# Counting edges into three tables in turn, halving the searches, and moving divisions and mixtures one site up in a graph-network kernel

## The chip, the core and the metric

The kernel runs on one core of one Trainium2 chip. The core has a matrix engine (TensorE, PE in the profile), a vector engine (VectorE, DVE), an activation engine (ScalarE, ACT), a general engine (GpSimd, POOL) and a sync engine (SyncE, SP) that here only issues transfers. Each engine works through its own instructions in order and waits for the others by semaphores. GpSimd and SP also issue DMAs; all of them share 16 DMA engines. The metric is the device time of one execution in microseconds (us); less is better. Three runs of the kernel before took 736.06, 737.99 and 738.41 us.

## What is computed

Two graph layers on 384 nodes and 12672 edges, each on a normalised and rectified copy of x, each added back to x. The first is a masked attention of 16 heads; its mask is set edge by edge. The second is a relational convolution of two layers, and there the count of edges by relation and node divides the messages:

```python
h = jnp.maximum(_layernorm(x), 0.0)
x = x + attention(h, edge_index, edge_type_5, ...)     # q, k, v: two projections each; mask.at[src, dst].set(w[edge_type - 1])
h = jnp.maximum(_layernorm(x), 0.0)
x = x + rgcn(h, edge_index, edge_type_6, ...)

def _rgcn_conv(x, src, dst, edge_type, basis, comp, root, bias):
    W = jnp.einsum('rb,bio->rio', comp, basis)          # R = 6 relations, B = 4 bases
    h_all = jnp.einsum('ni,rio->rno', x, W)
    counts = jnp.zeros((R, n), x.dtype).at[edge_type, dst].add(1.0)
    norm = 1.0 / counts[edge_type, dst]
    msg = h_all[edge_type, src] * norm[:, None]
    agg = jax.ops.segment_sum(msg, dst, num_segments=n)
    return agg + x @ root + bias
```

`rgcn` projects h by `w_in` (1024 to 768), applies this twice, each time with a rectifier, a residual and a batch norm, and projects back by `w_out` with a layer norm. All data are float32.

## The kernel before

The kernel turns gathering and scattering into dense matrices. For every relation r it builds a matrix A[r] of 384 x 384 that counts the edges from each source to each destination; a column divided by its sum is the mean of the relation. For each basis b the matrix At[b] is the mixture of the six divided matrices with the weights `comp[r, b]`; the convolution then is the sum over b of (x times basis b) times At[b].

**Building the tables.** The edges come as 99 chunks of 128. Two edges of one chunk must not write the same cell in one DMA, so each chunk is searched on VectorE: `find_cells` (L232) loads the keys of some chunks, shifts them (`cells`, L241), and for each chunk compares the 128 keys with each other (L250, one instruction and one read of its accumulator, 0.27 us in all). It does so twice: `find(0, ...)` for the mask and `find(1, ...)` for the counts, each closed by two short instructions (L253, L255) that give the places of the writes. The chunks are dealt into pieces (`PIECES`); pieces 0 to 2 are searched ahead, pieces 3 to 9 at the steps 3, 6, 8, 10, 12, 14 and 16 of a generator, `edge_steps`. Its steps are called from the projections by `fill(1)` (L404, L483): step 3 in the last part of the first projection, step n + 4 in part n of the 16 later parts (four of each of q2, k, k2 and v). `find_cells` does the first search and returns the second as a function; L296 calls it on the spot.

GpSimd writes each chunk: `put_mask` (L260) into one of four mask tables, `put_count` (L264) into one of two count tables `atab` in DRAM, as a DMA that adds to what is there. Such a DMA has to wait until an earlier one on the same table has landed. Counts 0 to 10 go to table 0, the others in turn to both. From count 20 on nothing but counts is left on GpSimd (L300), and they run on through the attention into the second layer. `clear` (L270) fills a table's relations with zeros through SP ahead of that.

**The projections.** Each of the 16 parts makes 7 products of half the width (a scheme that saves an eighth product by sums of operands): per part VectorE makes four sums of weights for the next part (`prepare`, L371), then whatever `fill` brings, then adds products from PSUM (L496, L502, L504); the last product of a part, `rest`, runs two products into the next one, and it writes the bank `pa` that L502 reads. At the end of a projection `node_sum` makes four sums of the new operand (L364).

**The end of the attention.** At f + 2 == STEPS (L647) SP loads the input projection and five parts of the first two bases, and then A: for each relation a plain load from one table (SP for relations 0 and 1, GpSimd for the others) and a load from the other that adds (L658). `add_up(r)` (L330) sums the three blocks of rows of A[r] on GpSimd.

**The convolution.** Each layer runs over four bases (`for b in range(B)`, L832) and then the root (L875). In a basis TensorE runs three steps c of twelve matrix instructions (3.87 us), with the `rest` of the basis before after step 0 (1.94 us), and then four products (7.74 us). `go_between(l, b, c)` (L822) is called after each step and, as c = 4, at the basis' end; what runs there is looked up in `between` (L811). Two kinds of work stand there. `share(r)` (L335): one matmul with ones (two matrix instructions) gives the column sums, VectorE takes the maximum with 1 and the reciprocal (L340, L341), GpSimd multiplies A[r] (L342), then `add_up(r + 2)`. `mix(l, r, At, bs)` (L319): for r = 0 on ScalarE, else one VectorE instruction over 128 x 1152 per basis (L326). On VectorE the site's work of step 2 comes before the sums L853, L861 and L863 that empty the banks of the basis, and `weight_sums` of the next basis (L787, L789) comes after them and before the site c = 4. The first matmuls of the next basis write the bank that L861 reads; the third block of the root's first row writes the one that L853 reads.

Of the kernel before, what the change touches and what calls it, by code (L numbers as in the profile page):

```python
# [10 lines left out]
F32 = mybir.dt.float32  # L11
# [19 lines left out]
R = 6  # L31
# [20 lines left out]
def gnn_kernel(ctx: ExitStack, tc: tile.TileContext, out, x, edges, chunks, cols, rows, small,  # L52
# [114 lines left out]


    mtab = [tables.tile([MCELLS + P, 1], F32, name=f"mtab{i}") for i in range(MT)]
    atab = [tables.tile([ACELLS + P, 1], F32, name=f"atab{i}") for i in range(2)]  # L170
    keys_d = tables.tile([PAD, P], I32, name="keys_d")

    def edge_steps(ep, none, zero):
# [58 lines left out]
        def find_cells(p):  # L232

            r0, r1 = PIECES[p:p + 2]
            nt = tables_in(r0)
            keys, cells = [ep.tile([P, MT * 3, P], I32, tag=tag, name=tag, bufs=bufs)[:, :nt * (r1 - r0)]
                           for tag, bufs in (("keys", 3), ("cells", 1))]
            nc.sync.dma_start(keys.rearrange("p (j c) n -> p j (c n)", j=nt),
                              keys_d.rearrange("(j c) n -> j (c n)", j=MT)[None, :nt, r0 * P:r1 * P]
                              .to_broadcast([P, nt, (r1 - r0) * P]))  # L240
            nc.vector.tensor_scalar(cells, keys, 3, None, ALU.logical_shift_right)  # L241

            def rounds(v):
                return v.rearrange("p (j c) -> p j c", j=MT)[:, :nt, r0:r1]

            def find(i, row, mine, times, least):
                for n in range(nt * (r1 - r0)):
                    c = n // (r1 - r0) * PER + r0 + n % (r1 - r0)
                    same = ep.tile([P, P], F32, tag="same", name="same", bufs=2)
                    nc.vector.scalar_tensor_tensor(same, row[:, n, :], mine[:, c:c + 1], times,  # L250
                                                   ALU.is_equal, ALU.mult, accum_out=count[:, i, c:c + 1])
                off = ep.tile([P, MT, 3], F32, tag="off", name="off", bufs=2)[:, :nt, :r1 - r0]
                nc.vector.scalar_tensor_tensor(off, rounds(count[:, i, :]), least, rounds(away[:, i, :]),  # L253
                                               ALU.is_ge, ALU.mult)
                nc.vector.tensor_tensor(rounds(at[:, i, :]), off, rounds(own[:, i, :]), ALU.add)  # L255

            find(0, cells, own[:, 0, :], later, 1.0)
            return lambda: find(1, keys, key, weigh, 1024.0)
# [4 lines left out]

        def put_count():  # L264
            i, c = next(counts)
            nc.gpsimd.indirect_dma_start(atab[0 if i < 18 - DEALT else i % 2][:, :],  # L266
                                         bass.IndirectOffsetOnAxis(at[:, 1, c:c + 1], 0),
                                         count[:, 1, c:c + 1], None, compute_op=ALU.add)

# [18 lines left out]
            put_rounds(p)  # L288
        for find_more in rest:
            find_more()  # L290
        for step in range(2, 18):
            yield
            for i in {5: (0,), 6: (1,), 7: (2, 3), 8: (4, 5)}.get(step, (step - 4,) if 10 <= step < 16 else ()):
                clear(i // R, i % R)
            if step in (3, 6, 8, 10, 12, 14, 16):
                find_cells(max(3, step // 2 + 1))()  # L296
            for p in {8: (3,), 9: (4,), 10: (5,), 11: (6,), 16: (7, 8), 17: (9,)}.get(step, ()):
                put_rounds(p)
        yield
# [30 lines left out]
    def add_up(r):  # L330
        sums[r] = late.tile([P, N], F32, tag="sum", name="sum", bufs=2)
        nc.gpsimd.tensor_tensor(sums[r], A[:, r, 0, :], A[:, r, 1, :], ALU.add)
        nc.gpsimd.tensor_tensor(sums[r], sums[r], A[:, r, 2, :], ALU.add)

    def share(r):  # L335

        ps = next_bank("ps_cnt", ring[1:])
        nc.tensor.matmul(ps[:, :N], ones, sums[r], start=True, stop=True)
        rn = late.tile([P, N], F32, tag="rn", name="rn", bufs=2)
        nc.vector.tensor_scalar(rn, ps[:, :N], 1.0, None, ALU.max)  # L340
        nc.vector.reciprocal(rn, rn)  # L341
        nc.gpsimd.tensor_tensor(A[:, r], A[:, r], rn[:, None, :].to_broadcast([P, NT, N]), ALU.mult)  # L342
        if r + 2 < R:
            add_up(r + 2)


    with ExitStack() as inner:
# [284 lines left out]
        for g in range(STEPS + 1):  # L632
            f = g + LEAD
            if g < STEPS:
                turn_probs(g)
            if f < STEPS:
                exponents(f)
            if f - 1 in total:
                normalise(f - 1)
            if f + 1 < STEPS:  # L640
                scores(f + 1)
            if g == STEPS:
                ps_y = [next_bank("ps_y", range(7)) for _ in range(2)]
                multiply_o(ps_y[0], 0, 0, range(KD - 1))
            if g > 0:
                gather(g - 1)
            if f + 2 == STEPS:  # L647

                w_x = [act_tile("w_x") for _ in range(2)]
                for half in range(2):  # L650
                    nc.sync.dma_start(w_x[half], w_in[half])
                tabs = [tab[:ACELLS, :].rearrange("(t p r d) o -> r p t (d o)", p=P, r=R, t=NT) for tab in atab]
                w_first = [wload(basis[0, 0, part], "w_c") for part in range(3)]
                w_first += [wload(basis[0, 1, part], "w_c") for part in range(2)]
                for r in range(2):
                    nc.sync.dma_start(A[:, r], tabs[0][r])
                for r in range(R):
                    nc.gpsimd.dma_start(A[:, r], tabs[1][r], accum_op=ALU.add)  # L658
                    if r + 2 < R:
                        nc.gpsimd.dma_start(A[:, r + 2], tabs[0][r + 2])  # L660
                    if 0 < r < 3:
                        add_up(r - 1)
        soft_stack.close()
        xtp = ctx.enter_context(tc.tile_pool(name="xtp", bufs=2, side="right"))

# [100 lines left out]
    with tc.tile_pool(name="conv", bufs=1) as cp:  # L766
# [38 lines left out]
        def shares(*rs):  # L805
            return lambda: [share(r) for r in rs]

        def mixes(l, r, *bs):
            return lambda: mix(l, r, At, bs)

        between = {(0, 1, 1): shares(0), (0, 1, 2): shares(1),  # L811
                   (0, 2, 0): lambda: (mix(0, 0, At), share(2)), (0, 2, 1): mixes(0, 1, 0, 1), (0, 2, 2): mixes(0, 1, 2, 3),
                   (0, 2, 4): shares(3),
                   (0, 3, 0): mixes(0, 2, 0, 1), (0, 3, 1): lambda: (mix(0, 2, At, (2, 3)), share(4)),
                   (0, 3, 2): mixes(0, 3, 0, 1), (0, 3, 4): shares(5),
                   (0, 4, 0): mixes(0, 4, 0, 1), (0, 4, 1): mixes(0, 5, 0, 1), (0, 4, 2): mixes(0, 3, 2, 3),
                   (0, 4, 3): mixes(0, 4, 2, 3), (0, 4, 4): mixes(0, 5, 2, 3),
                   (1, 0, 0): mixes(1, 0, 0, 1, 2, 3)}
        for i in range(10):
            between[1, (i + 1) // 3, (i + 1) % 3] = mixes(1, 1 + i // 2, *((0, 1), (2, 3))[i % 2])  # L820
# [311 lines left out]
```

## Time and profile before

| | us |
|---|---|
| median of three runs | 737.99 |
| the profiled execution, its time | 735.77 |
| its span in the profile | 734.0 |
| TensorE busy | 713.5 (97%) |
| VectorE busy | 472.9 (64%) |
| GpSimd busy | 323.3 (44%) |
| projections of half width (16 parts) | 55.39 to 209.80 |
| attention proper | from 237.4 to 310.7 |
| convolution, layer 0: bases | 384.7 to 471.9 |
| last count issued by GpSimd | 385.05 |
| first matmul of a `share` | 413.55 |

A span is what the profile shows between the first and the last instruction; the time of the execution holds 1.8 us more around it. Busy shares are means over the whole: TensorE is busy nearly always, while VectorE is nearly full in some stretches (19.9 of 20 us between 445 and 465) and idle in others. Times in the text are from the start of the span. In the profile, a row of a timeline gives start, duration, engine, line, operation, output and inputs and, in brackets, how long the engine was idle before and who released it. A row of the waits gives who waited for whom, the total, how often, and the longest.

### The profile page before, as it was taken

The page shows a single profiled execution, that of the slowest core. Times are in us where ns is not written, and L with a number is a line of the kernel's source. Part 1 is how long each engine was busy: PE and PEld are TensorE (multiplying, and loading weights), DVE is VectorE, ACT ScalarE, POOL GpSimd, SP SyncE. Part 2 cuts the span into 40 slices and gives each one's busy share as a digit, 9 for nine tenths or more (in the row PEclk, how much of TensorE's full clock was granted, in tenths as well). Part 3 has the DMA queues.
Part 4 walks back from the last instruction along what each step waited for, and adds up shares of the span by engine and source line. Part 5 has one row for each costly group of instructions (what it writes and reads, how often), then busy time and mean ns, then how long its engine had stood idle before and what let it go on. Part 6 is the DMA issues. An engine that isn't in the chain of part 4 may idle for free.

```text
span 734.0 us, 8299 instructions
## 1 busy us (share of the span) xinstructions
PE 713.5 (97%) x3024; PEld 496.8 (68%) x3024; DVE 472.9 (64%) x1228; ACT 147.2 (20%) x338; POOL 323.3 (44%) x242
## 2 busy tenths in 40 slices
PE   8999989999999999999999999899999999999995
PEld 8759989999964444445995555555555555579943
DVE  6895897877504499625424779990187676506756
ACT  3201111111111477510131131100013111001100
POOL 1456777788886788587784454310000000030000
PEclk9999999999999999999999999999999999999999
DMA  7797766743447322623527953321003123700001
GB/s 296 261 346 231 221 182 209 212 148 115 116 119 240 59 1 2 215 0 47 127 2 169 312 163 129 129 83 46 0 1 107 66 85 129 271 29 1 1 29 57
DMA packets 40533, 90.96 MB, mean 124 GB/s; under 512 B 19644, under 2 KB 27680, under 8 KB 36270
## 3 DMA queue, kind: packets, MB, share of 16 engines
q1 hardware_dynamic: 18478, 79.62, 30.9%
q0 software_dynamic: 21008, 8.42, 10.4%
q10 hardware_dynamic: 1008, 2.41, 0.9%
q8 instruction: 23, 0.38, 0.2%
q14 instruction: 16, 0.13, 0.1%
HBM read 79.27 MB, written 11.16 MB: 123 GB/s over the span
## 4 chain that ended last, share of the span: by engine, by line
PE 86%; DVE 11%; ACT 1%; issue 1%; DMA 1%; DVEq 0%; ACTq 0%
PE ps_g L846 13%; PE ps_g L840 10%; PE ps_c L897 6%; PE ps_c L880 6%; PE ps_q L395 6%; PE ps_v L524 6%; PE ps_k L377 6%; PE ps_c L947 6%; PE ps_v L377 5%; PE ps_y L615 5%; PE ps_f L1054 4%; DVE same L250 3%; PE ps_q L377 3%; PE ps_x L377 3%; PE ps_o L608 2%; PE ps_s L563 2%
## 5 line engine op out<-in xcount | busy, mean ns | idle before, releaser
L266 POOL DMA_INDIRECT atab<-count,at x99 | 160.0, 1616 | 50.6 <-DMA atab<-count,at 26.2
L261 POOL DMA_INDIRECT mtab<-m_val,at x99 | 104.1, 1052 | 57.0 <-issue 24.4
L1041 POOL TENSOR_TENSOR x_sb<-x_sb,room 128x1024 f32<-128x1024 f32 x3 | 7.0, 2347 | 158.1 <-DMA room<-in_rows 158.1
L326 DVE SCALAR_TENSOR_TENSOR At<-A,small_sb,At 128x1152 f32<-128x1152 f32 x40 | 62.9, 1635 | 0.0
L840 PE MATMUL ps_g<-T,S 128*128 128x384 f32 x144 | 49.1, 486 | 0.0
L846 PE MATMUL ps_g<-w_c,XT 128*128 128x384 f32 x144 | 48.0, 487 | 0.0
L846 PE MATMUL ps_g<-w_c,XN 128*128 128x384 f32 x144 | 47.6, 486 | 0.0
L897 PE MATMUL ps_c<-At,H 128*128 128x384 f32 x144 | 46.6, 486 | 0.0
L395 PE MATMUL ps_q<-hT,w_q 128*128 128x384 f32 (+1 forms) x160 | 41.8, 422 | 1.4 <-ACT hT L90 1.4
L524 PE MATMUL ps_v<-w_v,v 128*128 128x512 f32 x96 | 41.9, 594 | 0.0
L840 PEld LDWEIGHTS ps_g<-T,S 128*128 128x128 f32 x144 | 27.4, 190 | 19.1
L897 PEld LDWEIGHTS ps_c<-At,H 128*128 128x128 f32 x144 | 27.4, 190 | 19.1
L846 PEld LDWEIGHTS ps_g<-w_c,XN 128*128 128x128 f32 x144 | 27.4, 190 | 19.1
L846 PEld LDWEIGHTS ps_g<-w_c,XT 128*128 128x128 f32 x144 | 27.2, 190 | 19.2 <-DVE H L861 0.6
L395 PEld LDWEIGHTS ps_q<-hT,w_q 128*128 128x128 f32 x160 | 28.5, 190 | 14.1 <-ACT hT L90 1.7
L377 PE MATMUL ps_k<-T,S 128*128 128x192 f32 x192 | 35.8, 330 | 0.0
L615 PE MATMUL ps_y<-w_o,attT 128*128 128x512 f32 x80 | 35.0, 595 | 0.0
L576 DVE CUSTOM_DVE_ANT_0 s<-ps_s,mask 128x384 f32<-128x384 f32 x48 | 24.5, 548 | 15.4 <-PE ps_s L563 15.4
L342 POOL TENSOR_TENSOR A<-A,rn 128x1152 f32<-128x1152 f32 x6 | 19.4, 3236 | 31.7 <-DVE rn L341 31.7
L524 PEld LDWEIGHTS ps_v<-w_v,v 128*128 128x128 f32 x96 | 18.0, 190 | 22.6 <-issue 22.6
L377 PEld LDWEIGHTS ps_k<-T,S 128*128 128x128 f32 x192 | 32.7, 194 | 0.0
L1054 PE MATMUL ps_f<-w_out,XN 128*128 128x512 f32 (+1 forms) x84 | 31.1, 531 | 0.0
(250 smaller groups left out, 1316.6 us busy)
## 6 DMA issues: line engine op xcount, KB each, us to landing
w_c<-in_basis SPq DMA_DIRECT2D x24, 768.0 KB, 6.2
atab<-zero SPq DMA_DIRECT2D x12, 576.0 KB, 8.2
A<-atab POOLq DMA_DIRECT2D x10, 576.0 KB, 9.8
w_c<-in_root SPq DMA_DIRECT2D x6, 768.0 KB, 5.5
w_q<-in_wq SPq DMA_DIRECT2D x4, 1024.0 KB, 11.8
w_q<-in_wiq SPq DMA_DIRECT2D x4, 1024.0 KB, 10.1
w_k<-in_wk SPq DMA_DIRECT2D x4, 1024.0 KB, 7.0
w_k<-in_wik SPq DMA_DIRECT2D x4, 1024.0 KB, 6.2
```

The lines of the kernel that those rows point to most:

```text
L261: nc.gpsimd.indirect_dma_start(mtab[c // PER][:, :], bass.IndirectOffsetOnAxis(at[:, 0, c:c + 1], 0), m_val[:, c:c + 1], None)
L266: nc.gpsimd.indirect_dma_start(atab[0 if i < 18 - DEALT else i % 2][:, :], bass.IndirectOffsetOnAxis(at[:, 1, c:c + 1], 0), count[:, 1, c: ...
L326: nc.vector.scalar_tensor_tensor(At[:, b], A[:, r], w, At[:, b], ALU.mult, ALU.add)
L377: nc.tensor.matmul(ps, a[:, k, :], b[:, k, :], start=start and k == 0, stop=(k == 3), skip_group_check=not start)
L395: nc.tensor.matmul(ps[o][:, c], wt_[:, k, o * P:(o + 1) * P], src[:, k, c], start=(k == 0 and c.start == 0), stop=(k == KD - 1 and c.stop ...
L524: nc.tensor.matmul(ps, v[:, k, t * P:(t + 1) * P], w[k // 4][:, k % 4, :], start=(k == 0), stop=(k == KD - 1))
L615: nc.tensor.matmul(ps, attT[:, k, t * P:(t + 1) * P], w_o[half][k // 4][:, k % 4, :], start=(k == 0), stop=(k == KD - 1))
L840: nc.tensor.matmul(ps, x[:, c], y(c), start=start and c == 0, stop=(c == 2), skip_group_check=not start)
L846: nc.tensor.matmul(ps, block(XT, n, i)[:, c], w[c][:, i, o * HC:(o + 1) * HC], start=(first and c == 0), stop=(c == 2 and (i == 1 or ps is ...
L880: nc.tensor.matmul(pr[o], w[k // 2][:, k % 2, o * P:(o + 1) * P], XT[:, k, :], start=(k == 0), stop=(k == KC - 1 and l == L - 1))
L897: nc.tensor.matmul(pr[o], H_[:, b, n, o * P:(o + 1) * P], At[:, b, n, :], start=False, stop=(b == B - 1 and n == NT - 1))
L1054: nc.tensor.matmul(p, XT[:, k, t * P:(t + 1) * P], w[k // 2][:, k % 2, c0:c1], start=(k == 0), stop=(k == KC - 1))
```

## The change

Three things are changed. Counts from 11 to 92 go in turn to three tables, the last six to two of them; the third table is cleared like the others, at the steps 10 to 15, two clears in each. All six plain loads of A now come from the third table through SP, and both other tables are added by GpSimd, twelve loads in all (`add_tables`), ten of them dealt between the additions and `share`s. The second search of a piece is kept and called one step later. In the first layer of the convolution the sites of the `share`s and `mix`tures are moved one basis earlier.

```diff
-    atab = [tables.tile([ACELLS + P, 1], F32, name=f"atab{i}") for i in range(2)]
+    atab = [tables.tile([ACELLS + P, 1], F32, name=f"atab{i}") for i in range(3)]
...
         def put_count():
             i, c = next(counts)
-            nc.gpsimd.indirect_dma_start(atab[0 if i < 18 - DEALT else i % 2][:, :],
+            tab = atab[0 if i < 18 - DEALT else i % 3 if i < EC - 6 else i % 2]
+            nc.gpsimd.indirect_dma_start(tab[:, :],
...
+        rest = []
         for step in range(2, 18):
             yield
-            for i in {5: (0,), 6: (1,), 7: (2, 3), 8: (4, 5)}.get(step, (step - 4,) if 10 <= step < 16 else ()):
+            if rest:
+                rest.pop()()
+            for i in {5: (0,), 6: (1,), 7: (2, 3), 8: (4, 5)}.get(step, (step - 4, step + 2) if 10 <= step < 16 else ()):
                 clear(i // R, i % R)
             if step in (3, 6, 8, 10, 12, 14, 16):
-                find_cells(max(3, step // 2 + 1))()
+                rest.append(find_cells(max(3, step // 2 + 1)))
...
+    def add_tables(*rs):
+        for r, i in rs:
+            nc.gpsimd.dma_start(A[:, r], tabs[i][r], accum_op=ALU.add)
+
     def share(r):
...
         nc.gpsimd.tensor_tensor(A[:, r], A[:, r], rn[:, None, :].to_broadcast([P, NT, N]), ALU.mult)
+        add_tables(*{0: ((3, 1), (4, 0)), 1: ((5, 0), (4, 1)), 2: ((5, 1),)}.get(r, ()))
         if r + 2 < R:
             add_up(r + 2)
...
-                for r in range(2):
-                    nc.sync.dma_start(A[:, r], tabs[0][r])
                 for r in range(R):
-                    nc.gpsimd.dma_start(A[:, r], tabs[1][r], accum_op=ALU.add)
-                    if r + 2 < R:
-                        nc.gpsimd.dma_start(A[:, r + 2], tabs[0][r + 2])
-                    if 0 < r < 3:
-                        add_up(r - 1)
+                    nc.sync.dma_start(A[:, r], tabs[2][r])
+                add_tables((0, 0), (1, 0), (0, 1), (2, 0), (1, 1))
+                add_up(0)
+                add_tables((3, 0), (2, 1))
+                add_up(1)
...
-        between = {(0, 1, 1): shares(0), (0, 1, 2): shares(1),
-                   (0, 2, 0): lambda: (mix(0, 0, At), share(2)), (0, 2, 1): mixes(0, 1, 0, 1), (0, 2, 2): mixes(0, 1, 2, 3),
-                   (0, 2, 4): shares(3),
-                   (0, 3, 0): mixes(0, 2, 0, 1), (0, 3, 1): lambda: (mix(0, 2, At, (2, 3)), share(4)),
-                   (0, 3, 2): mixes(0, 3, 0, 1), (0, 3, 4): shares(5),
-                   (0, 4, 0): mixes(0, 4, 0, 1), (0, 4, 1): mixes(0, 5, 0, 1), (0, 4, 2): mixes(0, 3, 2, 3),
-                   (0, 4, 3): mixes(0, 4, 2, 3), (0, 4, 4): mixes(0, 5, 2, 3),
+        between = {(0, 0, 2): shares(0), (0, 0, 4): shares(1),
+                   (0, 1, 0): lambda: mix(0, 0, At), (0, 1, 1): lambda: (share(2), mix(0, 1, At, (0, 1))),
+                   (0, 1, 2): mixes(0, 1, 2, 3), (0, 1, 4): shares(3),
+                   (0, 2, 0): mixes(0, 2, 0, 1), (0, 2, 1): mixes(0, 2, 2, 3), (0, 2, 2): shares(4),
+                   (0, 2, 4): lambda: (share(5), mix(0, 3, At, (0, 1))),
+                   (0, 3, 0): mixes(0, 3, 2, 3), (0, 3, 1): mixes(0, 4, 0, 1), (0, 3, 2): mixes(0, 4, 2, 3),
+                   (0, 3, 4): mixes(0, 5, 0, 1), (0, 4, 1): mixes(0, 5, 2, 3),
```

## The prediction

> **What bounds the kernel now.** I read the page first. TensorE is busy for 713.5 of 734.0 us, so the change adds or removes no work on the engine that sets the end (it only moves six small matmuls): it can gain what TensorE waits, at most some 20 us, and it can lose by making TensorE wait elsewhere. The second view is the list of waits, TensorE alone (us in total, times, longest):
>
> ```profile
> PE ps_k L377 <- DVE k L502: 4.3, 3, 2.9
> PE ps_c L880 <- DVE H L853: 2.2, 1, 2.2
> ...
> PE ps_v L377 <- DVE v L502: 1.1, 1, 1.1
> ...
> PE ps_q L377 <- DVE q L502: 0.3, 1, 0.3
> ```
>
> Two places concern the change: the projections (L502, behind the searches) and the end of the first layer's fourth basis (L853, behind the mixtures). Third, the timeline of TensorE around the longest wait, then of VectorE (start, duration, idle before):
>
> ```profile
> 101.48 1.46 PE L377 MATMUL ps_k<-T,S 128*128 128x192 f32 x8
> 105.86 2.61 PE L377 MATMUL ps_k<-T,w_k 128*128 128x192 f32 x8 [2.92 <-DVE k L502]
> 108.26 2.14 PE L377 MATMUL ps_k<-T,S 128*128 128x192 f32 x8
> 110.24 1.46 PE L377 MATMUL ps_k<-hT,w_k 128*128 128x192 f32 x8
> ```
>
> ```profile
> 95.89 0.95 DVE L241 TENSOR_SCALAR cells<-keys 128x1536 int32<-128x1536 int32 x1
> ...
> 104.24 0.17 DVE L255 TENSOR_TENSOR at<-off,own 128x12 int32<-128x12 f32 x1
> 104.33 0.95 DVE L364 TENSOR_TENSOR T<-hT,T 128x768 f32<-128x768 f32 x1
> ...
> 105.46 0.34 DVE L502 TENSOR_TENSOR k<-k,ps_k 128x192 f32<-128x192 f32 x1
> ```
>
> One product takes 1.30 us from start to start; a whole search holds VectorE from 95.89 to 104.33, the sum at L502 stands behind it, and TensorE may not write its bank before that. After the wait, two products run slow (2.4 and 2.0 us instead of 1.30). Fourth, GpSimd's timeline, and the page's row of the counts (busy, mean ns, idle before): they go out 1.86 us apart (14.84 us for the eight gaps before the last, at 385.05) unless one waits for an earlier count of its own table, 26.2 us in all:
>
> ```profile
> 298.15 1.55 POOL L266 DMA_INDIRECT atab<-count,at x1 [0.30 <-issue]
> 300.74 1.55 POOL L266 DMA_INDIRECT atab<-count,at x1 [1.04 <-DMA atab<-count,at]
> 306.61 1.57 POOL L266 DMA_INDIRECT atab<-count,at x1 [4.32 <-DMA atab<-count,at]
> ```
>
> ```profile
> L266 POOL DMA_INDIRECT atab<-count,at x99 | 160.0, 1616 | 50.6 <-DMA atab<-count,at 26.2
> ```
>
> Last, both engines where the divisions and mixtures run: a mixture takes 1.33 us alone (ten from 480.02 in 15.64, one of them held up by 2.3), and 3.8 beside a division of GpSimd.
>
> ```profile
> 470.65 5.00 DVE L326 SCALAR_TENSOR_TENSOR At<-A,small_sb,At 128x1152 f32<-128x1152 f32 x2
> ...
> 470.82 3.63 POOL L342 TENSOR_TENSOR A<-A,rn 128x1152 f32<-128x1152 f32 x1 [8.34 <-DVE rn L341]
> ...
> 476.18 2.31 PE L880 MATMUL ps_c<-XT,w_c 128*128 128x384 f32 x6 [2.19 <-DVE H L853]
> ```
>
> **What the Trainium skill says.** "SBUF — State Buffer", section "Who interferes with whom": a VectorE instruction with two SBUF inputs and a GpSimd instruction that reads SBUF exclude each other, and the loser waits out the whole instruction. The last fence agrees: two mixtures take 5.00 instead of 2.7 us. "DMA: Bandwidth & Descriptors", section "Rules for kernel authors": an accumulating DMA must wait for the earlier DMA on the same bytes; the 26.2 us above are such waits, and the loads of A will have them too. "TensorE: Matmul & The Clock Gate", section "What's actually happening": the array's clock falls to half after an idle window of about 3.4 us. Here 2.92 us of waiting were already followed by slow products, so I charge a pause of 2 to 3 us some 1 to 2 us more.
>
> **The change, part by part.** The sum is made in the profiled execution (735.77 us, span 734.0; 2.2 us below the median of 737.99).
>
> *Searches split.* 16 parts of 7 products of 1.30 us need 145.6 us; TensorE takes 154.4 (55.39 to 209.80), so 8.8 us are lost: 5.7 listed above, the rest slow products and pipeline ends. After the change a part has at most, on VectorE: two late node sums 1.74, four weight sums 2.56, the longest half (0.95 + 12 x 0.273 + 0.45) 4.65, one node sum 0.87, L496 and L502 0.6; together 10.4 us after the part's start, and 8 to 9.5 in most parts. TensorE needs L502 11.7 us after that start (nine products). The cover is thus over 1 us everywhere but in the first part, where I find it just reached. Second halves come a part (9.1 us) later: GpSimd takes up the counts of rounds 9, 12, 15 and 18 at 95.8, 118.6, 142.3 and 163.4, and their halves end near 88, 108, 125 and 146, so it waits for none. **-8.8 us.** The mask does not move along, since GpSimd's pace sets it: ready at 232.6, wanted at 229.6 (238.4 - 8.8); scores of the next pair need those banks only 8.5 us later, so that is covered.
>
> *Third table.* Six more clears on SP, 0.43 us each, in parts whose loads are four ahead: nothing. The write traffic (3.5 MB within 45 us) meets engines at 0.46 to 0.85 of their share: nothing. From the count at 223.62 to the last at 385.05 there are 75 gaps; at 1.875 us they take 140.6 of the 161.4. A turn of three forgives a landing of 5.6 us after the start instead of 3.7. Of the landings that the waits give (4 to 6 us mostly, 8.5 and 9.5 when the 3.8 MB of loads start at 299) about 5 us of waiting stay: last count at 369.3. While the last six run, by turns of two, the loads from the third table start (3.5 MB). The burst at 299 cost 6.5 us (298.15 to 312.13 is 14.0 us for four gaps), so this one costs 0 to 6.5; I take 3.6. With 3.1 us to land (385.05 to 388.1) the last count lands at 376 (372.4 to 379) instead of 388.1.
>
> *Loads of A.* Twelve accumulating loads instead of six. The six plain ones go to SP, behind the five early basis loads (the last buffer for these comes free near 346) and ahead of a basis load whose own buffer is free only near 392; so they hold up nothing there. On GpSimd, a load that waits holds all behind it, additions and divisions too. To the first sum lead two in a row, each behind the other (5 and 5.5 us; between the 3.9 of a load alone and the 6.4 of the first one now), the issues and two additions (2.1): 13 us (10.5 to 15). The first sum is there at 389 (383 to 394). Its matmul moves from 413.7 to the old 396.3, now 387.5. TensorE's queue runs in order, so it would stop there: **+1.5 us** (0 to 6.5). The second, 8 us later, is in time.
>
> *Divisions and mixtures.* Counts of instructions stay; the same six divisions, six pairs of additions and 20 mixtures begin some 25 us earlier. But before L853 of the fourth basis stand now 16 mixtures and 5 reciprocals, where before 10 and 5 stood. From L863 of the first basis (396.1 plus the stop of 1.5) VectorE has, without a gap: three times weight sums 4.38, five times 3.06 for reciprocals, three times 1.49, 16 mixtures of 1.33, seven short sums of 0.48: 13.1 + 15.3 + 4.5 + 21.3 + 3.4 = 57.6 us. Beside GpSimd it loses some 2.3 us for each division (5) and 1.2 for each pair of additions (3 to 4): 15 us (11 to 18; the old stretch, 404.55 to 475.58, shows 14). So L853 ends at 397.6 + 72.6 = 470.2, not at 476.05. TensorE, which would be at its wait at 465, stops about 3.5 us before the third basis (L861 late) and 1 to 3 us later on, so it runs at VectorE's pace; for slow products after these stops I add 1. It resumes near 471.2 instead of 476.18: **-5.0 us in all**. Of the 8.8 us plus the 2.8 lost around L853 today (2.2 listed), this stage keeps 6.6 for itself. The four mixtures that are left do not matter: the next reader of At starts 23 us later. ACT's four mixtures of the first relation (4.7 us) wait for a division that ends near 396 and start at 403. Later loads and the second layer are untouched.
>
> 735.77 - 5.0 = 730.8 in this execution; on the median 737.99 - 5.0 = **733.0 us**, with 730 to 736 for this case alone.
>
> **The rivals.** *Both waits go and nothing comes for them* (L853 in time, no stop at the first sum): 8.8 + 2.8 = 11.6, so 726.4. For it speaks that VectorE idles 7.5 us between 405 and 425 today and gets work there; against it the 16 mixtures before L853. It holds if the overlap with GpSimd costs under 9 us. *Nothing measurable*: a first sum near 394, a stop of 6.5, leaves 0: 738. *Slower, by the tables being late*: if three DMAs in flight just land later, or the loads of the third table hold the last six, the last count lands at 388 as before, the first sum is there at 401, and TensorE stops 13.5 us at a site that before lay 12 us behind its sum. L853 without any stop would end at 396.1 + 72.6 = 468.7, 7.4 earlier than now; 7.4 - 13.5 = -6, so 744. The point from which it decides is a first sum after 395, that is a last landing after 382. Against it: 26.2 us of waits that name exactly those DMAs, and 4 bytes a row that fill no queue (1 to 3 GB/s between 260 and 300). For it: landings of 9.5 us beside a burst.
>
> **How the numbers follow.** A measurement tells 0.3% from no change here, 2.2 us. Chances: the forecast 0.50, the full gain 0.22, nothing 0.10, slower 0.18. Below 735.8 lie nearly all of the first two: 0.67; within 0.3% 0.15; slower 0.18. The range goes from the full gain, 726.5, to 740; above it stays most of the slower case, below it little.
>
> **What would show it.** Right: no waits of L377 for L502; the last count near 369 to 374; a short or no wait of TensorE at L338; VectorE without gaps from 398 to 470 and waits for L861 or L853 of a few us. Wrong: waits at L502 left over; a wait at L338 over 7 us (the slower rival); VectorE done with L853 before 466 (the full gain).

## The result: slower, with a new stop ahead of the first division

The changed kernel takes 749.15 us (median of 4 runs, 748.21 to 750.86), the kernel before 737.02 beside it (736.05 to 738.41). The ratio is 1.0158, 95% interval 1.0133 to 1.0183. 733.0 had been predicted, with a range up to 740. The profiled execution of after took 748.78 us, its span is 746.6; that of before 735.77 and 734.0. In some groups of the runs further below TensorE also waited in the projections for ScalarE's evictions (16.5 us in the list of e10), and the kernel before was slow beside them too (741.9 to 759.7 us in that group), so a run is compared by its ratio to the kernel before beside it, and a stage by its own length.

### Where the time went

TensorE's starts at the borders of the stages, in us from the start of the span:

| | before | after | shift |
|---|---|---|---|
| end of the projections (first product of the second V, L534) | 209.80 | 200.96 | -8.8 |
| third group of scores | 254.47 | 250.41 | -4.1 |
| convolution, first product | 384.52 | 380.36 | -4.2 |
| products behind the first division's site | 396.13 | 405.03 | +8.9 |
| third basis | 426.45 | 441.50 | +15.1 |
| first use of At (L905) | 499.61 | 512.31 | +12.7 |

From there on both kernels run alike. Of the 8.8 us won in the projections, 4.8 are lost at the scores, and the convolution's first layer takes 131.95 us instead of 115.09. The list of waits of after, TensorE alone (us in total, times, longest), has none for the searches any more, and three that the kernel before does not have:

```profile
PE ps_cnt L347 <- POOL sum L338: 11.5, 1, 11.5
PE ps_g L854 <- DVE H L869: 3.9, 1, 3.9
PE ps_s L573 <- DVE top L586: 2.6, 1, 2.6
```

The timeline of TensorE in after shows the first two of them (start, duration, work, idle before and releaser):

```profile
403.59 1.65 PE L347 MATMUL ps_cnt<-sum,ones 128*128 128x384 f32 x2 [11.46 <-POOL sum L338]
405.03 5.44 PE L848 MATMUL ps_g<-T,S 128*128 128x384 f32 x12
```

```profile
436.75 0.81 PE L347 MATMUL ps_cnt<-sum,ones 128*128 128x384 f32 x2
441.50 5.83 PE L854 MATMUL ps_g<-w_c,XT 128*128 128x384 f32 x12 [3.94 <-DVE H L869]
```

and the third, ahead of the second group of scores:

```profile
239.71 3.08 PE L573 MATMUL ps_s<-k,q 64*128 64x384 f32 x8 [2.57 <-DVE top L586]
```

The share matmul of relation 0 stands at its new site, three sites ahead of the old one (396.13 and 413.55 in the times of before), and TensorE stops there until GpSimd has the sum. Work behind a stop is slow: twelve matmuls take 5.44 and 5.83 us instead of 4.03, and eight of the scores 3.08 instead of 1.56. The stretch as a whole is told by one row of the windows for each kernel (window, its length, busy time of PE, its weight loads, DVE, ACT and POOL, granted clock, DMA share, GB/s); before, then after:

```profile
384.50:499.60 115.10, 112.89 (x350) 65.90 (x349) 92.16 (x84) 16.51 (x29) 47.53 (x30) 1.00 0.53 158
```

```profile
380.40:512.30 131.90, 116.50 (x349) 67.93 (x348) 90.08 (x84) 16.49 (x29) 50.46 (x32) 0.94 0.57 142
```

The 16.8 us are 13.2 more of waiting (15.4 against 2.2) and 3.6 more of busy time at a granted clock of 0.94. VectorE and ACT run as many instructions as before (84 and 29), GpSimd two more.

Why the sum is late is read from GpSimd's timeline of after:

```profile
378.11 1.55 POOL L268 DMA_INDIRECT atab<-count,at  x1 [3.65 <-DMA atab<-count,at]
379.96 1.55 POOL L268 DMA_INDIRECT atab<-count,at  x1 [0.30 <-issue]
384.34 1.65 POOL L268 DMA_INDIRECT atab<-count,at  x1 [2.83 <-DMA atab<-count,at]
388.20 2.68 POOL L342 DMA_DIRECT2D A<-atab  x2 [2.21 <-DVE T L803]
395.23 1.27 POOL L342 DMA_DIRECT2D A<-atab  x1 [4.35 <-DMA A<-atab]
397.38 2.57 POOL L342 DMA_DIRECT2D A<-atab  x2 [0.87 <-issue]
401.48 0.98 POOL L337 TENSOR_TENSOR sum<-A 128x384 f32<-128x384 f32 x1 [1.53 <-DMA A<-atab]
402.54 0.99 POOL L338 TENSOR_TENSOR sum<-sum,A 128x384 f32<-128x384 f32 x1
```

The last count goes out at 384.34, hardly earlier than the 385.05 of before. From there to the end of the first sum it is 19.2 us, where before took 16.1. Two loads follow each other in both chains; in before they are a plain load on SyncE and one adding load:

```profile
388.11 0.91 SPq L656 DMA_DIRECT2D A<-atab  x2
```

```profile
392.67 1.36 POOL L658 DMA_DIRECT2D A<-atab  x1 [6.07 <-DVE T L795]
...
399.05 1.00 POOL L332 TENSOR_TENSOR sum<-A 128x384 f32<-128x384 f32 x1 [2.15 <-DMA A<-atab]
```

The change took the plain load out of the chain, but a second adding load came in: 7.0 and 6.3 us in after, 4.6 and 6.4 in before. The page's row of the counts says that the third table took away no waiting in all (28.2 us at its end, 26.2 before):

```profile
L268 POOL DMA_INDIRECT atab<-count,at x99 | 159.2, 1608 | 54.1 <-DMA atab<-count,at 28.2
```

The timelines say where it went. In the counts by turns the waits fell from 23.5 to 9.3 us. In the first eleven counts they rose from 2.8 to 12.0, where SyncE's timeline of after now has two clears at a time:

```profile
94.93 1.66 SPq L273 DMA_DIRECT2D atab<-zero  x2
...
104.03 0.91 SPq L273 DMA_DIRECT2D atab<-zero  x2
```

and in the last six, beside the six loads of A, from 0 to 6.9. The early waits also make the mask late: its last part is written by 238.86 (before by 232.64), and TensorE stops 2.57 us for it ahead of 239.71.

### The profile page after: what moved, and what is told of

Its sections match the earlier page's. It is cut to its first block, busy times and chain, and to the rows that moved or that the text cites. A ratio compares the mean times of both kernels' runs of the same rounds, so it can differ in the third digit from the quotient of the medians.

```text
span 746.6 us, 8319 instructions
## 1 busy us (share of the span) xinstructions
PE 715.6 (96%) x3024; PEld 497.8 (67%) x3024; DVE 470.8 (63%) x1228; ACT 146.9 (20%) x338; POOL 324.2 (43%) x244
## 5 line engine op out<-in xcount | busy, mean ns | idle before, releaser
L268 POOL DMA_INDIRECT atab<-count,at x99 | 159.2, 1608 | 54.1 <-DMA atab<-count,at 28.2
L854 PE MATMUL ps_g<-w_c,XT 128*128 128x384 f32 x144 | 49.6, 500 | 3.9 <-DVE H L869 3.9
L905 PE MATMUL ps_c<-At,H 128*128 128x384 f32 x144 | 46.6, 486 | 0.0
L534 PE MATMUL ps_v<-w_v,v 128*128 128x512 f32 x96 | 42.5, 602 | 0.0
L905 PEld LDWEIGHTS ps_c<-At,H 128*128 128x128 f32 x144 | 27.4, 190 | 19.0
L534 PEld LDWEIGHTS ps_v<-w_v,v 128*128 128x128 f32 x96 | 18.4, 194 | 23.4 <-issue 22.3
L910 DVE TENSOR_TENSOR XN<-XN,XT 128x384 f32<-128x384 f32 x6 | 3.3, 555 | 47.3 <-ACT XN L931 47.3
```

What stands on the lines that cost most here:

```text
L268: nc.gpsimd.indirect_dma_start(tab[:, :], bass.IndirectOffsetOnAxis(at[:, 1, c:c + 1], 0), count[:, 1, c:c + 1], None, compute_op=ALU.add)
L534: nc.tensor.matmul(ps, v[:, k, t * P:(t + 1) * P], w[k // 4][:, k % 4, :], start=(k == 0), stop=(k == KD - 1))
L854: nc.tensor.matmul(ps, block(XT, n, i)[:, c], w[c][:, i, o * HC:(o + 1) * HC], start=(first and c == 0), stop=(c == 2 and (i == 1 or ps is ...
L905: nc.tensor.matmul(pr[o], H_[:, b, n, o * P:(o + 1) * P], At[:, b, n, :], start=False, stop=(b == B - 1 and n == NT - 1))
```

## The experiments

Each run's number is its ratio to the kernel before, with the 95% interval in brackets. "Convolution" below is the time from its first product to the first use of At, read from one profiled execution of each kernel: 115.1 us before, 131.95 after.

### The parts alone

The split alone (the second half is called one step later):

```diff
+        rest = []
...
+            if rest:
+                rest.pop()()
...
-                find_cells(max(3, step // 2 + 1))()
+                rest.append(find_cells(max(3, step // 2 + 1)))
```

> The kernel before with the split of the searches alone (two tables, old sites). Theory A (the third table's extra clears lengthen the landings of the early counts and so delay the mask): no extra clears here, so the mask is ready near 232.6 as before, TensorE has no wait at L502 and none for the mask, and the stage's gain is kept: 737 - 8.8 = 728 us. Rival B (the second half, one part later, holds GpSimd's counts up and delays the mask): the mask is ready near 237 here too and TensorE waits 2 to 3 us for it: 732 to 733 us.

0.9974 (0.9950 to 0.9999). The time of neither theory came (728, or 732 to 733, would be ratios of 0.988 to 0.995). The waits for the searches are gone and the mask is in time. In the profiled execution ScalarE held TensorE for 2.6 us in the projections, so the convolution starts 4.0 us earlier than before and not 8.8; it then takes 118.0 us instead of 115.1, with a wait of 2.8 for VectorE at the fourth basis. So most of what the split had won there is given back where VectorE was the next one late.

The moved sites alone, with two tables (the table `between` of after, nothing else):

> The kernel before with the moved sites alone (two tables, whole searches). Theory A (the moved sites need tables that two or three tables in turn cannot deliver in time): the first sum ends near 401, its matmul now stands near 396, so TensorE stops some 5 us there; the first division stands on GpSimd behind loads that end near 421, so ScalarE and VectorE hold TensorE for another 8 to 12 us: 747 to 753 us. Rival C (the sites are harmless, the third table's longer chain of adding loads is what stops TensorE): the stop is under 5 us and the time stays within 737 to 741 us.

1.0110 (1.0038 to 1.0182). The convolution takes 125.7 us. From the list of waits of this kernel:

```profile
PE ps_cnt L338 <- POOL sum L333: 9.9, 2, 9.1
```

The loss comes with the sites, whichever way the counts are written. The third table alone, with the sites of before and whole searches:

> The kernel before with the third table alone: its clears, its turn, the loads through SP and the adding loads, but whole searches and old sites. Theory A: counts 2 to 7 wait 1 to 2.5 us each, the mask comes 4 us later but TensorE is not there before it (no wait, or under 1 us); the last count goes out near 384; the first sum near 403 is in time for a matmul at 413: 735 to 738 us. Rival C (the longer chain of adding loads itself costs): a wait at the first sum's matmul or at the mixtures, 741 us or more.

0.9997 (0.9969 to 1.0024): by itself it neither gains nor loses. Its first sum ends at 402.4, but the share stands at 420 there. And the changed kernel with the sites of before:

> The changed kernel with the old sites (split and third table stay). Theory A: the projections keep their 8.8 us, the mask gives 4 to 5 back, and the first sum near 403 is in time for a matmul near 409: 737 - 4 = 733 us (731 to 735). Rival C (the third table costs in the convolution even at the old sites): a stop at the first sum, 738 us or more.

0.9953 (0.9927 to 0.9979). Against 1.0158 this puts the moved sites at 2% of the time, some 15 us. The time is as expected, its way is not: the last count went out only at 391.51 and the first sum ended at 416.6, so that even at the old sites TensorE stopped 3.8 us at shares.

### The two costs that had been put at nothing or too low

The clears of the third table over nine steps instead of two in each of six:

```diff
-            for i in {5: (0,), 6: (1,), 7: (2, 3), 8: (4, 5)}.get(step, (step - 4, step + 2) if 10 <= step < 16 else ()):
+            for i in {2: (12,), 3: (13,), 4: (14,), 5: (0,), 6: (1,), 7: (2, 3), 8: (4, 5), 9: (15, 16), 16: (17,)}.get(step, (step - 4,) if 10 <= step < 16 else ()):
```

> The changed kernel with the third table's six clears moved to steps 2, 3, 4, 9 and 16, so that one clear, not two, goes out beside each of the counts 2 to 10. Theory A (the doubled clears lengthen those counts' landings): their waits fall from 12.6 us in sum to 4 or less, the mask is ready near 234 and TensorE does not wait for it; the last count and the first sum come some 4 us earlier, and so does everything after the stop at the first sum: 4 us less than the changed kernel's 749, 745 us. Rival D (the third table makes the early counts land late in another way than by its clears, or the clears cost as much wherever they stand): waits over 8 us, the mask near 238, 749 us.

1.0121 (1.0080 to 1.0162). The waits of the first eleven counts fall from 12.0 to 1.7, the mask is ready at 235.6 without a stop, and the convolution starts at 376.23 instead of 380.36. Yet the time falls by less than these 4 us (the intervals of the two ratios overlap), as TensorE comes earlier to a sum that is little earlier, at 402.05 instead of 403.54: the counts by turns, begun earlier, now wait 14.6 us instead of 9.3.

```profile
PE ps_cnt L347 <- POOL sum L338: 14.1, 1, 14.1
PE ps_g L854 <- DVE H L869: 3.8, 1, 3.8
```

So the doubled clears are what the mask was late by, and most of that lay in the shadow of the later stop. Next, only two plain loads of A ahead, the other four behind the counts on GpSimd's queue:

> The changed kernel with only the loads of relations 0 and 1 from the third table ahead of the last counts; the other four go out on GpSimd behind the counts and behind the first two adding loads. Theory A (the burst of six loads holds the last six counts): counts 93 to 98 wait under 2 us instead of 6.9, the last one goes out near 379 instead of 384.3, the first sum comes some 4 us earlier and TensorE's stop there falls from 11.5 to 6 to 8 us: 745 us. Rival E (six counts in turn between two tables are slow by themselves): the waits stay at 5 us or more and the stop at 11 us.

1.0177 (1.0141 to 1.0213): the expectation missed. The last six counts wait 3.0 instead of 6.9 us and the last goes out at 381.76, but the four loads then lie beside the adding loads, and from that count to the end of the first sum it takes 24.4 us instead of 19.2. The stop is 14.0.

### What the sites cost when the sum is in time

The adding loads of relations 0 and 1 are left out:

```diff
-                add_tables((0, 0), (1, 0), (0, 1), (2, 0), (1, 1))
+                add_tables((2, 0))
```

> Leaves out the adding loads of tables 0 and 1 into relations 0 and 1 (so those two relations hold a third of their edges); everything else as in the changed kernel. Theory A (the first sum's lateness is what the moved sites cost): the first sum stands right behind the last count, at about 388, its share matmul is reached without a stop, the 11.5 us go, and with them the slow clock after; the wait for the late VectorE before basis 2 (3.9) may stay. About 736 us, ratio to before 0.995 to 1.00. Theory B (divisions and mixtures among the bases cost by themselves, through VectorE and GpSimd): stops of the same sum appear elsewhere in the convolution, and the time stays above 743, ratio above 1.007.

1.0102 (1.0015 to 1.0188), where at most 1.00 was expected, and the run cannot decide: TensorE had been held in the projections and came to the site at 409, when even the full chain could have been done. Only the stage is of use, 118.4 us with a wait of 4.2 for VectorE. With the spread clears it was tried again:

> The changed kernel with spread clears, and without the adding loads of tables 0 and 1 into relations 0 and 1 (these hold a third of their edges). Theory A (the late sum is nearly all of what the moved sites cost): the convolution is entered at about 376, the first sum ends at 390 to 393 right behind the last counts, the stop at the first share is 0 to 2.5 us instead of 14.1, the late VectorE costs 4; convolution from its first product to its first use of At 118 to 120 us instead of 133.6; about 730 to 732, ratio 0.991. Theory B (early divisions and mixtures cost by themselves): convolution above 125, ratio above 1.00.

0.9963 (0.9947 to 0.9979), against 1.0121 with these loads: the late sum, with the loads themselves, costs 1.6%, some 11.7 us, and the convolution is 11.6 us shorter. The list of waits and the timeline of TensorE in this kernel:

```profile
PE ps_g L854 <- DVE H L869: 5.6, 1, 5.6
...
PE ps_cnt L347 <- POOL sum L338: 1.1, 1, 1.1
```

```profile
426.22 6.01 PE L854 MATMUL ps_g<-w_c,XT 128*128 128x384 f32 x10 [5.62 <-DVE H L869]
```

The first sum ends at 388.7, the stop is 1.1. But the convolution takes 122.0 us, more than the 118 to 120 expected and more than before: four mixtures ahead of L869 take 9.4 us beside GpSimd and make VectorE late at the third basis. So the early sites win nothing even with the sum at hand.

Every site one later than the change put it, with relation 0's adding loads first, and then with each relation's loads ahead of its sum:

```diff
-{(0, 0, 2): shares(0), (0, 0, 4): shares(1), (0, 1, 0): lambda: mix(0, 0, At),
+{(0, 0, 4): shares(0), (0, 1, 0): shares(1), (0, 1, 1): lambda: mix(0, 0, At),
...
```

> The changed kernel with its clears spread, relation 0's adding loads first, and every division and mixture one site later than the change put it (the first share at the end of basis 0, at about 399.5). Theory A: the first sum ends at 398 to 401, so the stop at the first share is 0 to 2.5 us instead of 11.5 to 14; a wait for the late VectorE of 1 to 4 us stays before basis 1 or 2; about 733 us, ratio 0.993. Theory B (early mixtures cost by themselves): above 740.

> The changed kernel with spread clears, each relation's adding loads ahead of its sum, and every site one later than the change put it (first share at about 399, second at about 403). Theory A: first sum at 397 to 401, second at 404 to 408; stops of together 1 to 5 us instead of 14.1, late VectorE 2 us; convolution 116 to 121 us; about 730 to 733, ratio 0.992. Theory B: above 740.

1.0083 (0.9998 to 1.0168) and 1.0152 (1.0117 to 1.0187): both missed. The stops stayed, 7.4 us at the second share in the first run and 14.3 at three shares in the second, whose first sum ended only at 406.4 although its last count went out at 383.4, before that of after.

### What makes the sum late once more

> The three tables with spread clears and late mixtures (730.19 before this call), with both adding loads of relation 0 issued ahead of relation 1's and relation 2's. Theory A (the queue of adding loads works at some 200 GB/s, so a 576 KB load is some 2.9 us of it, and relation 0 waits for loads it doesn't need): the second load of relation 0 lands 3 to 6 us earlier, the first sum ends at 401 to 404 instead of 407.9, the wait of 2.4 at the first share goes; about 727 us, ratio 0.985. Rival (a landing is a fixed latency of about 7 us, whatever is queued): the first sum ends at 404 to 408 and the time stays within 1 us of 730.

> Three tables, spread clears, the sites of before with the mixtures of relations 3 to 5 late, and the adding loads of relation 0, then of relation 1, each ahead of its sum, then those of relations 2 and 3. Theory A: first sum at 400 to 404, second at 406 to 410, no stop at a share, no wait for VectorE, convolution 112 to 114 us instead of 116.6; about 726 to 728, ratio 0.985. Rival: the adding loads take the same time in any order (7 us each landing), ratio 0.989 to 0.991.

0.9914 (0.9830 to 0.9998) and 0.9966 (0.9947 to 0.9985): in e14's profile relation 0's loads ahead of the others' did not make its sum earlier (it ended at 410.15), as the rival said. All runs together point to something else. From the issue of the last count to the end of the first sum, by when SyncE starts the basis weights that wait for the buffers of the first basis:

| | weights from 404 on | weights at 392 to 401 |
|---|---|---|
| two tables | 16.2 (e2), 16.5 (e18) | 20.0 (e16) |
| three tables | 19.2 (after), 18.9 (e3), 19.8 (e5), 19.0 (e11), 19.4 (e12), 19.3 (e17) | 25.1 (e4), 24.7 (e8), 25.0 (e14), 23.0 (e15) |

Counted from the last count, the weights come after 16 us or more in the left column and after 4 to 11 in the right. (Left out: e6 and e7, in whose chains further plain loads lie, four and six of them, and e9 and e13, which have no adding loads there. In before and in the split alone they start at 400.84 and 396.87, when the chain is nearly through: 16.1 and 16.5. In e10 a wait of 5.6 for the plain loads makes it 22.5.) GpSimd's timeline of e8, and SyncE's:

```profile
395.12 1.27 POOL L342 DMA_DIRECT2D A<-atab  x1 [4.36 <-DMA A<-atab]
397.26 2.57 POOL L342 DMA_DIRECT2D A<-atab  x2 [0.87 <-issue]
406.81 0.98 POOL L337 TENSOR_TENSOR sum<-A 128x384 f32<-128x384 f32 x1 [6.97 <-DMA A<-atab]
```

```profile
393.69 1.62 SPq L80 DMA_DIRECT2D w_c<-in_basis  x3
```

The wait of 6.97 us is 1.53 in after. What each queue moved from 396 to 404 (packets, MB, and the packets' time as a share of 16 engines' span; q1 has SyncE's loads, q0 GpSimd's) shows the collision itself, in e8 and then in after:

```profile
q1 hardware_dynamic: 412, 2.30, 74.6%
q0 software_dynamic: 302, 0.44, 32.1%
```

```profile
q0 software_dynamic: 953, 1.39, 105.4%
```

Beside the weights the adding loads move a third of what they move alone; e4 has 0.46 MB of them beside 2.20 of weights from 403 to 411. VectorE, which stands still in the stop of after, is not the reason: in e12 it is busy for 6.2 of the 8 us from 392 to 400, the adding loads move 1.37 MB, and the chain takes 19.4. The Trainium skill, "DMA: Bandwidth & Descriptors", section "Rules for kernel authors", says that spreading loads over several issuing engines adds no bandwidth, as all run on the same 16 DMA engines and interleave; these figures agree. So an earlier TensorE frees its weight buffers earlier, and the weights it calls for hold up the sum that it will wait for. In after the stop itself kept them away, until 411.14.

### Versions that gain

The sites of before, but the mixtures of relation 3 (and behind them those of 4 and 5) in the root instead of the fourth basis:

```diff
-(0, 3, 2): mixes(0, 3, 0, 1), (0, 3, 4): shares(5),
-(0, 4, 0): mixes(0, 4, 0, 1), (0, 4, 1): mixes(0, 5, 0, 1), (0, 4, 2): mixes(0, 3, 2, 3),
-(0, 4, 3): mixes(0, 4, 2, 3), (0, 4, 4): mixes(0, 5, 2, 3),
+(0, 3, 4): shares(5),
+(0, 4, 0): mixes(0, 3, 0, 1), (0, 4, 1): mixes(0, 3, 2, 3), (0, 4, 2): mixes(0, 4, 0, 1),
+(0, 4, 3): lambda: (mix(0, 4, At, (2, 3)), mix(0, 5, At, (0, 1))), (0, 4, 4): mixes(0, 5, 2, 3),
```

e7 does this with two tables, the split, all plain loads on SyncE and the adding loads dealt; e8 with three tables, the split and spread clears; e16 on the kernel before with the split and nothing else. e12 is e8 with the old mixtures.

> A version meant to be faster: two tables, split searches, all six plain loads through SP, adding loads of relations 4 and 5 behind the first two divisions, old sites, and the mixtures of relation 3 after the fourth basis instead of in it. Theory A (what the split wins is lost where mixtures and divisions stand too early for VectorE and for the tables): no waits at L502, none for the mask, none at the first sum, none at the end of the fourth basis; 8.8 + 2.8 us less than before on the same chip, ratio 0.984. Rival F (VectorE is the bound in this stage wherever the mixtures stand): waits of 2 us or more for its sums at the end of a basis or before the first mixture's reader, ratio 0.992 or more.

> The changed kernel with the clears spread and the late sites of the run before. Theory A: the third table neither helps nor harms once nothing waits for it: ratio to the kernel before within 0.4% of the run with two tables, about 0.986. Rival C (the longer chain of adding loads costs): a stop at the first sum of 3 us or more, ratio 0.99 or more.

> The changed kernel with the sites of before and its clears spread over nine steps: the pair to the run with the sites of before and the clears as changed (0.9953). Theory A (clears two at a time beside the first counts cost TensorE some 3 to 4 us at the mask, which nothing hides when no stop follows): no wait at the scores of the second part, ratio 0.990, about 731. Rival (the late mixtures, not the spread clears, made the difference between 0.9953 and 0.9879): ratio 0.995, about 734.5.

> The kernel before with the searches split and the mixtures of relation 3 moved from basis 3 into the root, nothing else: two tables, its own loads, its own sites for the divisions. If the third table is worth nothing by itself once the searches are split and VectorE is freed at basis 3: the wait of 2.8 for H at basis 3 is gone, 8.8 is kept of the projections; about 731, ratio 0.990 to 0.993. If the third table's earlier sum is needed: ratio 0.995 to 0.998, with a stop at a share.

e7: 0.9919 (0.9891 to 0.9946), e8: 0.9879 (0.9846 to 0.9913), e12: 0.9958 (0.9889 to 1.0027), e16: 0.9989 (0.9965 to 1.0012). e8, 730.19 us (729.14 to 730.36), beats both kernels. In its list of waits there is one of 2.4 us left for the first sum and none for VectorE, where e12 still has one of 2.0 for L861. The wide interval of e12 doesn't tell what the late mixtures are worth; the stage does. With the sum in time, the convolution takes 116.2 us with the old mixtures (e12) and 112.2 with the late ones (e10, and e17 below, which has the loads of e12). e16 fails as its last count goes out at 388.24 and its sum collides with the weights: stops of 3.5 and a wait of 4.7 for VectorE behind them.

e7 was expected at 0.984: the six plain loads through SyncE stand in its chain, from 394 on, and TensorE stops 4.8 us for the first sum.

Last, two weight loads of the third basis behind the first sum, by a copy of one column of it on SyncE's queue; on e8 and on e16:

```diff
...
+            if (l, b) == (0, 1):
+                nc.sync.dma_start(late.tile([P, 1], F32, tag='gate', name='gate'), sums[0][:, :1])
...
```

> Three tables, spread clears, the sites of before with late mixtures (730.19 in an earlier call, first sum ended at 408.9 with a wait of 7.0 for its last adding load), and SyncE's two weight loads of basis 2 held behind the first sum by a copy of one column of it. If the weight loads beside the adding loads are what makes the first sum late: it ends at 401 to 404, the wait of 2.4 at the first share goes, convolution 112 to 114 us, ratio 0.984 to 0.987, about 727. If the adding loads take their time by themselves: first sum at 406 to 409 as before, ratio 0.988 or more (more, if basis 2 then waits for its weights).

> Two tables, the searches split, the mixtures of relation 3 late (0.9989 in an earlier call, first sum ended at 408.2, stops of 3.5 at shares and 4.7 for a late VectorE), and the same two weight loads held. If the collision makes the first sum late: it ends at 401 to 404, the stops go, ratio 0.990 to 0.994. If not: 0.998 as before.

0.9822 (0.9778 to 0.9865), the lowest ratio of the study, and 0.9920 (0.9895 to 0.9945), as good as e7. Both convolutions run without a wait of TensorE, 112.2 and 112.4 us; the row of the windows of e17:

```profile
390.00:503.00 113.00, 113.00 (x355) 66.89 (x354) 87.09 (x84) 16.49 (x29) 45.11 (x28) 1.00 0.63 160
```

But in both profiled executions TensorE had been held in the projections and left the first basis only at 407 and 405, when the sum was ready; the copy held nothing there. Nor can the ratios be put down to it, as a late TensorE takes the collision away by itself: e10, without the copy and held up in the same way, has a convolution of 112.2 us and no wait too. Whether the copy helps is not shown. That the weights cost the sum 4 to 6 us rests on the table and the queues above.

## Why the prediction was wrong

**The step that failed is the time of the first sum**, and with it the stop at the first division: +1.5 us (0 to 6.5) in the prediction, 11.46 measured, as the sum came at 403.5 instead of 389. All that was forecast behind it took the tables to be complete by then.

**Searches split: -8.8 us predicted, -8.84 measured**, and no wait for them is left. This part was right.

**"Six more clears on SP ... : nothing"** failed first in time. The sum left out that the early counts, which all go to table 0, land beside the clears of the other two tables: two clears of 576 KB at a time made the first eleven counts wait 9.2 us more, and in e5 they wait 1.7 in all. The step "the mask does not move along" then fell: it came 6 us later and TensorE lost 4.8 us, 2.6 of waiting and most of the rest in slow work behind it. With the clears over nine steps the mask is still 3 us later than before, but TensorE doesn't stop for it.

**The last count, predicted at 372.9, came at 384.34.** Three terms were too small: GpSimd came to the later counts 4.4 us late (the loads of the mask tables' V go out at 222.81 instead of 218.41), 9.3 us of waits stayed instead of 5, and the loads of A held the last six by 6.9 instead of 3.6. Together that is 12.0 us, for a last count that came 11.4 late. The third turn itself came near the sum, with 14 us fewer waits in its own counts.

**The chain to the first sum**, 13 us from the landing (with 3.1 to land, 16.1 from the issue), was 19.2: the two adding loads in a row took 7.0 and 6.3 us (388.20 to 395.23 to 401.48) instead of 5 and 5.5. The late last count and this chain make up the 14.5 us. The rival that ended slower had named the place and the point ("a first sum after 395, that is a last landing after 382") and gave 744; I gave it 0.18. Its shift of 6 us falls 6.7 short of the 12.7 at the first use of At; by estimate some 2.5 of this are a first sum at 403.5 instead of its 401, and 3.6 the slow work, which it did not charge.

**The wait before the third basis** was right in its place: about 3.5 us predicted, 3.9 measured, for the same sum (L861 of before is L869 of after). That the size agrees is in part luck, as VectorE was to have no gap from 398 on and stood still until the first sum; with the sum in time the wait is 4.2 (e9) and 5.6 (e13). The 1 to 3 us later on did not come. With the sum in time the stage would have taken 118.9 us by the prediction (from 384.52 - 8.8 to 499.61 - 5.0); the two runs with the sum in time show 118.4 and 122.0. So the length of the part on VectorE held within some 3 us, and what failed is when the tables are complete.

**The clock.** The Trainium skill, "TensorE: Matmul & The Clock Gate", section "What's actually happening", puts the fall to half clock behind an idle window of about 3.4 us. Here a wait of 2.57 us was already followed by eight matmuls in 3.08 instead of 1.56 us. I had charged the stops in the convolution 1 us in all; they cost 3.6.

## What to carry to other kernels

Before work is moved up to an earlier site, its longest chain of transfers is priced from the last write to the first use, with each transfer at the length it has beside the others that will then be under way; a queue that runs in order pays every microsecond that is missing there, and pays again at the slow clock. A stage that is made faster calls for its next weights earlier, and these may lie on the same DMA engines as the chain it will wait for. Clears, too, are traffic: in pairs beside small accumulating writes they delayed these by 9 us, dealt out singly by none (1.7 us in all, 2.8 before).

## What was not expected of the hardware

From the issue of relation 0's second accumulating load (576 KB) to the sum behind it, it took 6.3 us in after (395.23 to 401.48) and 11.7 in e8 (395.12 to 406.81), where three weight loads of 768 KB had begun 1.4 us before it; the order of the adding loads among themselves changed nothing (19.0 us for the whole chain in e11, 19.4 in e12). And a stop can protect a chain: the long stops inside the first basis, in after and e5, went with a chain of 19 to 20 us, while e4, e8, e14 and e15, which called for the next weights by 401, had 23 to 25.
